# Attention and FFN on one core: side work dealt over the four head groups of a batch, units that cannot begin passed over, and norms moved to ScalarE

## The chip, the core and the metric

The kernel runs on one core of a Trainium2 chip. A core has TensorE (PE in the profile; PEld is its weight load), VectorE (DVE), ScalarE (ACT), GpSimd (POOL) and SyncE (SP, which here only issues transfers). Each engine runs its own instructions in the order in which they were issued, and waits on semaphores for the others. The metric is the device time of one execution in microseconds (us), as the median of several runs.

## What is computed

The reference works on four batches of 1024 rows with 256 columns, in float32, and on a context of 77 rows for each batch:

```python
x = x + xattn(_layernorm(x), ctx, Wq, Wkv, Wout, bout)   # 16 heads of 16, causal after the 77 context rows
x = x + ffn(_layernorm(x), w_fc, b_fc, w_proj, b_proj)

# xattn: q = x @ Wq; k, v = split(concat(ctx, x) @ Wkv)
#        softmax(q k^T / 4, keys j <= i + 77) @ v, then @ Wout + bout
# ffn:   every linear layer rounds its input and its weight to 3 mantissa bits with one
#        exponent per 32 columns; gelu between w_fc (1024 hidden) and w_proj
```

The keys are 77 + 1024 = 1101 for each batch.

## The kernel before, in words

**Head groups.** The sixteen heads of a batch are worked in four groups of four, so there are 16 groups, `kk` 0 to 15; batch `b` is groups 4b to 4b+3. A group is cut into 14 pieces of keys against queries: five for the first 512 queries (512, 461, 333, 205 and 77 columns wide) and nine for the second (512 five times, then 461, 333, 205, 77). Each piece is done in two half-steps of two heads each, so a group has 28 half-steps (`half_step`, L918). A half-step computes the raw scores of the *next* group for its row maxima (L490 on TensorE into `s_ps`, L514 or L516 on VectorE) and the transposed scores of *this* group (L554 into `st_ps`), whose exponential ScalarE takes (L565, `pt`); on the diagonal GpSimd zeroes the masked part (L570). The product with V (`times_v`, L591, `av_ps`) follows one to two half-steps behind. PSUM has two buffers of `st_ps` and three of `s_ps`.

**Side work.** All else is cut into units that are issued between half-steps. A unit is a list of stages; the first is issued at once, the others a given number of half-steps later (`begin` and `tick`, L891 and L901; `LATER` is 3). The units are:
- for the next batch: `load_unit`; `stats_unit` (L144, L145); `root1_unit` (Newton steps for 1/std, L160 to L163, on GpSimd); `norm_unit` (one tile: scale rows, L349, then turn on TensorE, L358, and copy into `xT`); `mem_unit` for the context; `qk_unit` and `v_unit` (projections, L420 and L393) and `move_unit` (transfers of a staged Q or K, L438, on SP's queue);
- for the batch before: `divide_unit` (softmax sums, transfers and L659); `wout_unit` (output projection L688, residual L696, statistics); `root_unit`; `in_unit` (norm L736, rounding with L178, L185, L189, L200, L201, turn L749); `hidden_unit` (four tiles of the first FFN layer, L768 to L779); `out_unit` (rounding, turn L820, projection L828, residual L835);
- in batch 0 sixteen `weight_unit` instead (rounding and turning the FFN weights, turn L858).

`helper[0]` is GpSimd from the first score step until the last group, and VectorE outside: it does the Newton steps, both norms, the residual additions, the scaling by the softmax sums and half of the rounding.

**Who decides the order.** `run` (L945) gets the group's list of units, written out by hand for each group of a batch (L999 to L1038). Each unit has a guessed cost; the list's total, spread over the half-steps by their width, gives a share for each, and the head of the list is issued while the share lasts and the unit's `ready()` holds:

```python
while todo and share > 0 and ready(todo[0]):
    u = todo.popleft()
    share -= price(u)
    begin(u)
```

What is left over is carried to the next group. In a batch that has both a batch before and one after it, group 0 got `wout` of the first half, Q and all norms of the next batch; group 1 the `in` units and the first `hidden`; group 2 five V units, four `out` units and Q, with K carried in from the group before; group 3 the rest.

Of the kernel before, what the change touches and what calls it, by code (L numbers as in the profile page):

```python
# [9 lines left out]
F32 = mybir.dt.float32  # L10
# [7 lines left out]
P = 128  # L18
# [7 lines left out]
ICW = 512  # L26
# [17 lines left out]
def kernel(  # L44
# [101 lines left out]

    def inv_std(mv, rstd, t0, t1, engine):


        n = t1 - t0  # L150
        v = small.tile([P, n], F32, name="v")
        nc.vector.tensor_scalar(v, mv[:, t0:t1, 1], EPS, None, ALU.add)
        y = small.tile([P, n], F32, name="y")
        nc.vector.tensor_scalar(
            y.bitcast(I32), v.bitcast(I32), -0.5, float(0x5F3759DF), ALU.mult, ALU.add
        )
        e = small.tile([P, n], F32, name="e")
        def newton(step):
            def emit():
                engine.tensor_tensor(e, y, y, ALU.mult)  # L160
                engine.tensor_tensor(e, e, v, ALU.mult)
                engine.tensor_scalar(e, e, -0.5, 1.5, ALU.mult, ALU.add)
                engine.tensor_tensor(y if step < 2 else rstd[:, t0:t1], y, e, ALU.mult)  # L163
            return emit

        return [newton(step) for step in range(3)]
# [38 lines left out]
    mv1 = const.tile([P, TT, 2], F32, name="mv1")  # L205
    rstd1 = const.tile([P, TT], F32, name="rstd1")
    mv2 = const.tile([P, TT, 2], F32, name="mv2")
    rstd2 = const.tile([P, TT], F32, name="rstd2")

    with ExitStack() as actx:
# [99 lines left out]
        def stats_unit(b, it):  # L312
            def emit():
                stats(xn[b, it // HN][:, it % HN, :], mv1, b * NT + it)
            return cost(0.7, emit)

        rooted1 = set()

        def root1_unit(b, half):
            got = {}  # L320

            def start():
                t0, n = (0, NT) if half is None else (half * HN, HN)
                got["steps"] = inv_std(mv1, rstd1, b * NT + t0, b * NT + t0 + n, helper[0])

# [16 lines left out]
        def norm_unit(b, it):  # L342
# [3 lines left out]
            def scale_rows():  # L346
                held["xh"] += 1
                xh = work.tile([P, D], F32, name="xh")
                helper[0].tensor_scalar(  # L349
                    xh, xn[b, it // HN][:, it % HN, :], mv1[:, t, 0:1], rstd1[:, t : t + 1],  # L350
                    ALU.subtract, ALU.mult,
                )
                got["xh"] = xh
# [8 lines left out]

            scale_rows.ready = lambda: (b, it // HN) in rooted1 and held["xh"] < XH
            return cost(0.8, [scale_rows, turn])

        def mem_unit(b):
# [16 lines left out]

            fetch.ready = room("xh", XH)
            return cost(0.5, [fetch, turn])

        def v_unit(b, jt):
            def emit():
# [15 lines left out]
                )  # L404
            return emit

        def qk_unit(hh, which, part):

            def emit():
# [18 lines left out]
                projected[b] += lo + n == total  # L428
            return cost(1.0, emit)

        def move_unit(hh, which):

            def emit():
                into, n = (qTs, N) if which == "q" else (kTs, KEYS)
                GR = HPG * HD
                for i in range(2):
                    t = into[(hh * 2 + i) % NQK]
                    nc.sync.dma_start(out=t[0:P:2, :], in_=qk_st[which][i * GR : (i + 1) * GR, :])  # L438
                    if which == "q" and hh * 2 + i >= NQK:
                        nc.sync.dma_start(out=t[MXR:P:PAD, :], in_=t[MXR + 2 : P : PAD, :])  # L440
            return emit

        def batch_units(b):
# [6 lines left out]
            for half in range(2):  # L450
                units += [stats_unit(b, half * HN + i) for i in range(HN)]
                units += [root1_unit(b, half)]
                units += [norm_unit(b, half * HN + i) for i in range(HN)]
            return first, units + [mem_unit(b)]

        def v_units(b):
            return [v_unit(b, jt) for jt in range(NJ)]

# [252 lines left out]
        def root_unit(b, half):  # L711
            got = {}

            def start():
                got["steps"] = inv_std(
                    mv2, rstd2, b * NT + half * HN, b * NT + (half + 1) * HN, helper[0]
                )
# [11 lines left out]
        def in_unit(t):  # L729
            got = {}  # L730

            def quantize():
                done["begun"] += 1
                held["xq"] += 1
                xh = work.tile([P, D], F32, name="xh")
                helper[0].tensor_scalar(  # L736
                    xh, x2[t], mv2[:, t, 0:1], rstd2[:, t : t + 1], ALU.subtract, ALU.mult
                )
                got["xh"] = xh
# [20 lines left out]
        def hidden_unit(tiles):  # L760
# [23 lines left out]
            )  # L784
            return cost(1.4 * len(tiles), emit)

# [97 lines left out]
        late = deque()  # L884
        LATER = 3
        clock = [0]
        pending = []
# [57 lines left out]
        def run(kk, extras):  # L945
# [10 lines left out]
            for n in range(STEPS):  # L956
                for pair in range(2):
# [16 lines left out]
                    tick()  # L974
                    share = min(share + rate * length[n], 2.5)
                    if urgent and ready(urgent[0]):
                        begin(urgent.pop(0))
                    while todo and share > 0 and ready(todo[0]):
                        u = todo.popleft()
                        share -= price(u)  # L980
                        begin(u)
                if kk >= 0:
# [16 lines left out]
        for kk in range(last + 1):  # L999
            b, g = divmod(kk, NG)  # L1000
            f = b - 1
            extras, qs, loads, norms = [], [], [], []
            if kk % 2 == 0:
                if kk // 2 + 1 < pairs:
                    extras.append(move_unit(kk // 2 + 1, "k"))
                    qs = q_units(kk // 2 + 1)
            if g == 0 and b + 1 < B:
                loads, norms = batch_units(b + 1)
            vs = v_units(b + 1) if b + 1 < B else []
            if g == NG - 1:  # L1010
                urgent += [divide_unit(b, 0), divide_unit(b, 1)]
            if f >= 0:
                T = range(f * NT, (f + 1) * NT)
                if g == 0:
                    extras += loads + wout_units(f, 0) + qs + [root_unit(f, 0)]
                    extras += norms + wout_units(f, 1) + [root_unit(f, 1)]
                elif g == 1:
                    extras += [in_unit(t) for t in T[:HN]] + [hidden_unit(T[:HN])]
                    extras += [out_unit(T[0])] + [in_unit(t) for t in T[HN:]]
                elif g == 2:  # L1020
                    extras += merge(vs[:5], [out_unit(t) for t in T[1:HN]]) + qs
                    extras += [hidden_unit(T[HN:])]
                else:
                    extras += merge(vs[5:], [out_unit(t) for t in T[HN:]])
            else:
                n = -(-len(w_units) // NG)
                side = w_units[g * n : (g + 1) * n]
                if g == 0:
                    extras += loads + side[:2] + qs + norms + side[2:]
                else:  # L1030
                    extras += side[:2] + qs + side[2:]
                    extras += vs[:5] if g == 2 else vs[5:] if g == 3 else []
            if kk % 2 == 1:
                if (kk + 3) // 2 < pairs:
                    extras += k_units((kk + 3) // 2)
            if kk == last:
# [52 lines left out]
```

## Time and profile before

| what | value |
|---|---|
| runs shown | 1061.28, 1061.05, 1059.31 us; median 1061.05 |
| profiled execution | 1055.06 us, span 1053.3 us |
| mean granted TensorE clock in it | 0.95 |
| before the first exponential | 66.7 us |
| groups 0 to 3 | 50.2, 52.8, 51.6, 51.8 us |
| groups 4 to 7 | 57.3, 61.5, 70.3, 57.4 us |
| groups 8 to 11 | 58.6, 59.2, 70.3, 57.0 us |
| groups 12 to 15 | 48.5, 61.8, 57.3, 40.2 us |
| after the last exponential | 80.8 us |

A group is measured from its first exponential (L565) to the next group's first. In the page's slices each digit is the busy share of one fortieth of the span in tenths; the row PEclk is the TensorE clock that was granted, in tenths of full speed. A row of a window shows start and end, length, then the busy time of each engine with its instruction count, the granted clock, the share of the DMA engines and GB/s. A line of a timeline has start, duration, engine, line, operation, output and inputs; the bracket at its end is the time the engine was idle before it and what released it. Group lines have the total busy time, the mean in nanoseconds, and the idle time ahead of them.

### The profile page before, as it was taken

What the parts mean: (1) busy time and instruction counts of PE and PEld (TensorE: products, weight loads), DVE (VectorE), ACT (ScalarE), POOL (GpSimd) and SP (SyncE); (2) the same over time, 40 slices, a digit from 0 to 9 for tenths busy, and PEclk for the clock granted to TensorE, in tenths of its full rate; (3) what the DMA queues carried; (4) which work ended last, traced back from release to release, by engine and by line L of the source; (5) the groups of instructions that cost most, each with busy time, mean ns of one, the idle gap of its engine ahead of it and who ended that gap; (6) DMA issues with size and microseconds to landing.
All of it is one profiled execution on the core that took longest, in us unless ns stands there. A gap on an engine that the chain in (4) does not pass through costs nothing.

```text
span 1053.3 us, 21100 instructions
## 1 busy us (share of the span) xinstructions
PE 974.8 (93%) x8024; PEld 408.7 (39%) x8024; DVE 653.0 (62%) x2121; ACT 544.3 (52%) x790; POOL 412.3 (39%) x775
## 2 busy tenths in 40 slices
PE   4899899999998999999998999999999898999577
PEld 2353334343433434344443434434443333344233
DVE  3678657655674756457566566646566756552695
ACT  5145445555554565655553564565554564756233
POOL 1014513131327446334326546515333627343233
PEclk9889989999997999999998999999999999989686
DMA  3030101101320001100320101010022000001200
GB/s 104 22 81 21 36 12 40 43 18 35 87 53 16 22 1 35 33 17 21 84 73 13 31 6 30 17 32 19 26 70 63 13 1 13 12 17 49 69 20 21
DMA packets 36172, 36.31 MB, mean 34 GB/s; under 512 B 14067, under 2 KB 29747, under 8 KB 36070
## 3 DMA queue, kind: packets, MB, share of 16 engines
q1 hardware_dynamic: 34958, 33.90, 11.8%
q8 instruction: 63, 1.03, 0.4%
q10 hardware_dynamic: 1112, 1.06, 0.3%
q14 instruction: 39, 0.32, 0.1%
HBM read 16.58 MB, written 5.25 MB: 21 GB/s over the span
## 4 chain that ended last, share of the span: by engine, by line
PE 75%; DVE 11%; POOL 5%; DMA 3%; ACT 2%; issue 2%; SPq 1%; POOLq 0%; DVEq 0%; ACTq 0%
PE s_ps L490 32%; PE av_ps L591 15%; PE s_ps L420 6%; PE st_ps L554 5%; PE s_ps L393 3%; PE st_ps L768 3%; DVE jk L516 3%; PE s_ps L688 3%; PE s_ps L828 2%; DVE mx L514 2%; PE st_ps L773 2%; ACT pt L565 2%; POOL xh L349 1%; DMA xn<-in_x_dram 1%; DVE amaxh L178 1%
## 5 line engine op out<-in xcount | busy, mean ns | idle before, releaser
L565 ACT ACTIVATE pt<-st_ps 128x1024 f32<-128x1024 f32 (+4 forms) x448 | 353.4, 793 | 303.8 <-PE st_ps L554 272.7
L490 PE MATMUL s_ps<-kT,qT 32*128 32x512 f32 (+2 forms) x1736 | 490.1, 543 | 21.5 <-DVE mxp L516 11.4
L554 PE MATMUL st_ps<-qT,kT 32*128 32x512 f32 (+5 forms) x1792 | 488.1, 540 | 2.5 <-ACT pt L565 2.4
L570 POOL TENSOR_SCALAR_AFFINE_SELECT pt<-pt 128x254 f32<-128x254 f32 (+3 forms) x320 | 118.1, 372 | 437.6 <-ACT pt L565 435.1
L516 DVE CUSTOM_DVE_ANT_0 jk<-s_ps,tri,mx 128x77 bf16<-128x77 f32 (+3 forms) x372 | 174.1, 505 | 154.3 <-PE st_ps L554 119.4
L490 PEld LDWEIGHTS s_ps<-kT,qT 32*128 32x128 f32 x1736 | 187.9, 189 | 208.3 <-issue 63.9
L591 PE MATMUL av_ps<-pt,vaug 128*32 128x256 f32 (+7 forms) x3072 | 226.1, 369 | 2.4 <-POOL hq L201 1.2
L514 DVE TENSOR_REDUCE mx<-s_ps 128x1 f32<-128x512 f32 x248 | 159.8, 685 | 78.3 <-PE st_ps L554 75.7
L554 PEld LDWEIGHTS st_ps<-qT,kT 32*128 32x128 f32 (+1 forms) x1792 | 182.5, 186 | 15.1 <-ACT pt L565 11.1
L516 DVE CUSTOM_DVE_ANT_0 jk<-s_ps,tri 128x512 bf16<-128x512 f32 (+3 forms) x248 | 126.6, 550 | 94.4 <-PE st_ps L554 74.4
L591 PEld LDWEIGHTS av_ps<-pt,vaug 128*32 128x32 f32 (+1 forms) x3072 | 62.6, 109 | 198.0 <-issue 137.2
L201 POOL TENSOR_TENSOR hq<-h,magh 128x512 bf16<-128x512 f32 x64 | 68.3, 1070 | 34.5 <-DVE h L200 28.9
L200 POOL TENSOR_TENSOR h<-h,magh 128x512 f32<-128x512 f32 x40 | 41.9, 1047 | 36.6 <-DVE magh L189 36.1
L673 ACT COPY y<-s_ps 128x256 f32<-128x256 f32 x64 | 23.9, 373 | 51.2 <-PE s_ps L692 26.2
L779 ACT ACTIVATE h<-st_ps 128x1024 f32<-128x1024 f32 x32 | 32.7, 1023 | 29.2 <-PE st_ps L773 29.1
L768 PE MATMUL st_ps<-wfcT,xqT 128*128 128x512 bf16 x128 | 44.7, 436 | 1.8 <-ACT xqT L752 1.8
L178 DVE TENSOR_REDUCE amaxh<-h 128x16 f32<-128x512 f32 x64 | 42.7, 675 | 5.4 <-ACT h L779 5.4
L420 PE MATMUL s_ps<-xT,wk_sb 128*128 128x512 f32 (+1 forms) x96 | 38.9, 533 | 5.2 <-DVE mxp L516 5.0
L516 DVE DVE_READ_ACCUMULATOR2_ANT mxp<- 128x1 f32 x512 | 42.2, 82 | 0.0
L688 PE MATMUL s_ps<-wo_sb,o_pk 128*128 128x256 f32 x128 | 38.2, 421 | 1.9 <-DVE o_pk L659 1.9
L393 PE MATMUL s_ps<-wv,xT 128*128 128x256 f32 (+1 forms) x144 | 38.0, 396 | 0.0
L828 PE MATMUL s_ps<-wprT,hT 128*128 128x256 bf16 x256 | 35.2, 283 | 2.7 <-ACT hT L823 2.6
(101 smaller groups left out, 817.6 us busy)
## 6 DMA issues: line engine op xcount, KB each, us to landing
kT<-k_st SPq DMA_DIRECT2D x16, 275.2 KB
xn<-in_x_dram SPq DMA_DIRECT2D x16, 256.0 KB
qT<-q_st SPq DMA_DIRECT2D x16, 256.0 KB
o_pk<-o_st SPq DMA_DIRECT2D x32, 128.0 KB
rb<-rd SPq DMA_DIRECT2D x128, 32.0 KB
x<-in_x_dram SPq DMA_DIRECT2D x32, 128.0 KB
out_dram<-x SPq DMA_DIRECT2D x32, 128.0 KB
x<-in_L_ffn_w_fc_dram SPq DMA_DIRECT2D x8, 128.0 KB
```

What stands on the lines that cost most here:

```text
L201: nc.gpsimd.tensor_tensor(dst.rearrange("p (n k) -> p n k", k=QBLK), src3, magb, ALU.subtract)
L393: nc.tensor.matmul(vp[:nj, :], xT[b][:, k, jt * P : jt * P + nj], wv[:, k, :], start=(k == 0), stop=(k == KC - 1),)
L420: nc.tensor.matmul(pp[:, :n], w[:, k, hi * P : (hi + 1) * P], xT[b][:, k, first + lo : first + lo + n], start=(k == 0), stop=(k == KC - 1),)
L490: nc.tensor.matmul(sp[:, 0 : hi - lo], qTs[kk % NQK][rows, it * P : (it + 1) * P], kTs[kk % NQK][rows, lo:hi], start=True, stop=True,)
L514: nc.vector.tensor_reduce(into, sp[:, 0:w], axis=AX.X, op=ALU.max)
L516: nc.vector.tensor_tensor_reduce(junk.tile([P, ICW], BF16, name="jk")[:, 0:w], sp[:, 0:w], mask, 1.0, before, ALU.add, ALU.max, into)
L554: nc.tensor.matmul(st[:nj, e, : i1 - i0], kTs[kk % NQK][rows, t * P : t * P + nj], qTs[kk % NQK][rows, i0:i1], start=True, stop=True,)
L565: nc.scalar.activation(pt[:nj, :, :w], st[:nj, :, :w], AF.Exp, scale=scale)
L570: nc.gpsimd.affine_select(out=pt[:nj, :, :behind], in_=pt[:nj, :, :behind], compare_op=ALU.is_ge, fill=0.0, base=base, pattern=[[0, 2], [1 ...
L591: nc.tensor.matmul(acc[c * PAD : (c + 1) * PAD, off + lo : off + hi], vaugs[b % 2][:nj, t, v0 : v0 + PAD], pts[kk, n, c // 2][:nj, c % 2, ...
L688: nc.tensor.matmul(yp, o_pk[b, ic][:, k, it * P % ICW : it * P % ICW + P], wo_sb[:, k, :], start=(k == 0), stop=False,)
L768: nc.tensor.matmul(hp[:, n, :], xqT[t][:, k, :], wfcT[:, k, n * ICW : (n + 1) * ICW], start=(k == 0), stop=False,)
```

## The change

It has three parts.

1. **Norms.** Where the helper is GpSimd, both norms become one ScalarE activation with a per-row scale (1/std) and a per-row shift (-mean/std). The root units compute the shift with two more small instructions in their last step. Where the helper is VectorE (ahead of the first score step and after the last group has begun), the norm stays as it was, and the two instructions are still issued.
2. **`run`.** Among the first four units of the list the first that is ready is issued, and at most 1.3 of guessed cost is issued in a half-step. The guessed costs change. Q and K units got a `ready()` of their own, over a staging state for each of Q and K, and the norms and the context of the next batch wait for the last Q or K projection of the batch before, since `xT` has one buffer.
3. **The lists.** Group 0 of a batch now has K and Q of its second half of the heads, `wout` of the first half, the norms of the first half of the next batch, the first root and the first four `in` units, and `wout` of the second half; group 1 has the first `hidden`, the norms of the second half, two `out` units and the second root; group 2 has K and Q of the next batch's first heads, two `out` units, four `in` units and the second `hidden`; group 3 has all nine V units and four `out` units.

The diff, cut:

```diff
             def emit():
                 engine.tensor_tensor(e, y, y, ALU.mult)
                 engine.tensor_tensor(e, e, v, ALU.mult)
                 engine.tensor_scalar(e, e, -0.5, 1.5, ALU.mult, ALU.add)
                 engine.tensor_tensor(y if step < 2 else rstd[:, t0:t1], y, e, ALU.mult)
+                if step == 2:
+                    engine.tensor_tensor(e, mv[:, t0:t1, 0], rstd[:, t0:t1], ALU.mult)
+                    engine.tensor_scalar(shift[:, t0:t1], e, -1.0, None, ALU.mult)
...
+    def norm(dst, src, mv, rstd, shift, t):
+        if helper[0] is nc.vector:
+            nc.vector.tensor_scalar(
+                dst, src, mv[:, t, 0:1], rstd[:, t : t + 1], ALU.subtract, ALU.mult
+            )
+        else:
+            nc.scalar.activation(
+                dst, src, AF.Identity, bias=shift[:, t : t + 1], scale=rstd[:, t : t + 1]
+            )
...
-                helper[0].tensor_scalar(
-                    xh, xn[b, it // HN][:, it % HN, :], mv1[:, t, 0:1], rstd1[:, t : t + 1],
-                    ALU.subtract, ALU.mult,
-                )
+                norm(xh, xn[b, it // HN][:, it % HN, :], mv1, rstd1, shift1, t)
...
-            scale_rows.ready = lambda: (b, it // HN) in rooted1 and held["xh"] < XH
+            scale_rows.ready = lambda: (
+                (b, it // HN) in rooted1 and held["xh"] < XH and (not b or projected[b - 1] == 2 * KC)
+            )
...
-            return cost(1.0, emit)
+                staged[which] = hh, part + 1
+            emit.ready = lambda: normed[hh // KC] == NT + 1 and (
+                staged[which] == (hh, part) if part else staged[which] is None
+            )
+            return cost(1.5, emit)
...
-                helper[0].tensor_scalar(
-                    xh, x2[t], mv2[:, t, 0:1], rstd2[:, t : t + 1], ALU.subtract, ALU.mult
-                )
+                norm(xh, x2[t], mv2, rstd2, shift2, t)
...
-            return cost(1.4 * len(tiles), emit)
+            return cost(0.8 * len(tiles), emit)
...
+        AHEAD = 4
...
                     share = min(share + rate * length[n], 2.5)
+                    left = 1.3
                     if urgent and ready(urgent[0]):
                         begin(urgent.pop(0))
-                    while todo and share > 0 and ready(todo[0]):
-                        u = todo.popleft()
+                    while share > 0 and left > 0:
+                        u = next((u for u in list(todo)[:AHEAD] if ready(u)), None)
+                        if u is None:
+                            break
+                        todo.remove(u)
                         share -= price(u)
+                        left -= price(u)
                         begin(u)
...
                 if g == 0:
-                    extras += loads + wout_units(f, 0) + qs + [root_unit(f, 0)]
-                    extras += norms + wout_units(f, 1) + [root_unit(f, 1)]
+                    extras += loads + merge(qs, wout_units(f, 0)) + norms[0][: HN + 1]
+                    extras += norms[0][HN + 1 :] + [root_unit(f, 0)] + ins[:HN]
+                    extras += wout_units(f, 1)
                 elif g == 1:
-                    extras += [in_unit(t) for t in T[:HN]] + [hidden_unit(T[:HN])]
-                    extras += [out_unit(T[0])] + [in_unit(t) for t in T[HN:]]
+                    extras += [hidden_unit(T[:HN])] + norms[1][: HN + 1]
+                    extras += merge(outs[:2], norms[1][HN + 1 :]) + [root_unit(f, 1)]
                 elif g == 2:
-                    extras += merge(vs[:5], [out_unit(t) for t in T[1:HN]]) + qs
-                    extras += [hidden_unit(T[HN:])]
+                    extras += merge(qs, outs[2:HN]) + ins[HN:] + [hidden_unit(T[HN:])]
                 else:
-                    extras += merge(vs[5:], [out_unit(t) for t in T[HN:]])
+                    extras += merge(vs, outs[HN:])
```

`qs` is now the K units, the K move, the Q units and the Q move of the same pair of heads; before, the K units of a pair stood at the end of the list of the group before.

## The prediction

> **What bounds the kernel now.** I read the page first (busy shares, slices, the chain that ended last), then busy time in windows cut at the first exponential (L565) of each of the sixteen head groups, then the timeline where a window showed TensorE idle. From the page:
>
> ```profile
> PE 974.8 (93%) x8024; PEld 408.7 (39%) x8024; DVE 653.0 (62%) x2121; ACT 544.3 (52%) x790; POOL 412.3 (39%) x775
> PE   4899899999998999999998999999999898999577
> PEclk9889989999997999999998999999999999989686
> PE 75%; DVE 11%; POOL 5%; DMA 3%; ACT 2%; issue 2%; SPq 1%; POOLq 0%; DVEq 0%; ACTq 0%
> ```
>
> TensorE carries three quarters of the chain and its work is the same before and after, so only its stalls can be won: the idle slots, and the slices where the granted clock (PEclk) drops. Windows of head groups 4, 5, 6, 7, 8, 12 and 13 (start:end, length, busy us of PE, PEld, DVE, ACT, POOL, then granted clock):
>
> ```profile
> 273.10:330.40 57.30, 53.76 (x456) 21.53 (x452) 37.14 (x130) 27.11 (x41) 25.56 (x64) 0.93 0.22 58
> 330.40:391.90 61.50, 59.72 (x483) 23.08 (x478) 37.23 (x127) 33.77 (x50) 28.80 (x58) 0.95 0.06 17
> 391.90:462.20 70.30, 67.49 (x564) 28.80 (x556) 38.11 (x121) 40.68 (x58) 34.65 (x51) 1.00 0.11 28
> 462.20:519.60 57.40, 55.72 (x520) 24.51 (x512) 36.04 (x116) 31.34 (x46) 26.39 (x40) 1.00 0.09 25
> 519.60:578.20 58.60, 55.03 (x456) 21.66 (x452) 38.91 (x130) 27.09 (x41) 25.64 (x64) 0.92 0.25 67
> 764.70:813.20 48.50, 48.36 (x452) 19.78 (x444) 32.51 (x110) 25.73 (x36) 17.14 (x40) 1.00 0.27 70
> 813.20:875.00 61.80, 57.43 (x480) 22.09 (x476) 37.43 (x128) 33.19 (x45) 29.40 (x56) 0.92 0.02 7
> ```
>
> Group 12 is nearly stall-free (0.14 us idle, full clock). Its side work is two Q units at 1.93 us (the chain has 1.91 to 1.98) and four output projections at 1.2 (38.2 us / 32): 8.7. So a bare group is 48.5 - 8.7 = 39.8 us. Other TensorE prices: V unit 1.06 (38.0 / 36), hidden unit of four tiles 6.5 (its half-step lasts 8.1 instead of 1.6), out unit 1.75 (turn 0.7, project 1.05), norm turn 0.4, quantised turn 0.29, 77-column K part 0.4. Bare group plus its units, against its length, gives each group's stall: groups 0 to 3: 2.4, 7.0, 1.4, 2.3; 4 to 7: 7.2, 7.3, 2.4, 2.1; 8 to 11: 8.5, 5.0, 2.4, 1.7; 12 to 14: 0, 8.8, 3.5. Together 62 us: some 31 idle, some 21 lost to the clock ((1 - granted) x length), the rest half-steps stretched by VectorE. This is all the change can reach; the first 66.7 us and all after group 14 change little.
>
> Two places show how stalls arise (start, duration, engine, line, what; in brackets idle before and releaser):
>
> ```profile
> 317.95 4.83 POOL L349 TENSOR_SCALAR xh<-xn,mv,rstd 128x256 f32<-128x256 f32 x4
> 320.43 0.44 PE L358 MATMUL s_ps<-ident,xh 128*128 128x128 f32 x2 [0.78 <-POOL xh L349]
> 321.63 0.44 PE L358 MATMUL s_ps<-ident,xh 128*128 128x128 f32 x2 [0.76 <-POOL xh L349]
> 322.84 0.69 PE L358 MATMUL s_ps<-ident,xh 128*128 128x128 f32 x2 [0.76 <-POOL xh L349]
> ...
> 395.40 2.42 POOL L736 TENSOR_SCALAR xh<-x,mv,rstd 128x256 f32<-128x256 f32 x2
> 396.65 0.42 DVE L178 TENSOR_REDUCE amaxx<-xh 128x8 f32<-128x256 f32 x1 [0.71 <-POOL xh L736]
> 399.43 1.98 PE L420 MATMUL s_ps<-xT,wk_sb 128*128 128x512 f32 x4 [2.48 <-DVE mxp L516]
> ```
>
> First TensorE itself waits for GpSimd's norms, 1.2 us apiece. Then VectorE, in order, waits for a norm with maxima queued behind it; score buffers stay full and TensorE loses 2.48 us.
>
> **Part 1: the norms.** 48 norms (24 L349, 24 L736) leave GpSimd for ScalarE:
>
> ```profile
> L736 POOL TENSOR_SCALAR xh<-x,mv,rstd 128x256 f32<-128x256 f32 x24 | 29.2, 1219 | 0.0
> L565 ACT ACTIVATE pt<-st_ps 128x410 f32<-128x410 f32 x64 | 32.7, 515 | 28.8 <-PE st_ps L554 20.8 <-POOL pt L570 6.2 <-POOL hq L201 1.5
> L673 ACT COPY y<-s_ps 128x256 f32<-128x256 f32 x64 | 23.9, 373 | 51.2 <-PE s_ps L692 26.2 <-PE s_ps L831 24.7
> ```
>
> GpSimd loses 58 us and gains two small instructions in each of 12 roots: 24 at 0.28 us spacing, 7. ScalarE gains 48 activations. The near row, a 256-column copy, says 0.37 us each, 18 in all. [...] ScalarE then works some 55% of the time, so the amount is hidden behind TensorE. The built program has 14 table loads in both versions: none added.
>
> The price is the new wait. A norm needs the root's last step on GpSimd, now six instructions, 1.7 us, and is often issued in the same half-step. Behind it in ScalarE's queue stand the next exponential, and behind that TensorE, which has two score tiles. Group 4 has two such places. In its wide half-step 8 the root started one and a half half-steps earlier and two residual additions (0.72 each) share GpSimd: ScalarE waits 0 to 1.9 us, then runs three norms (1.7); the slack is about 1.2, so TensorE loses 0 to 2.4; I take 1.2. In half-step 10 the mask select L570 (0.42) stands ahead of the root step and itself waits for the exponential: wait 2.2, norms 1.1 to 2.2, cost 1 to 3, I take 2. Group 8 repeats this; group 12 has one place with a 1.27 us scaling ahead as well (2.5); groups 0 and 1 one each (1).
>
> **Part 2: a unit that cannot begin is passed over; even dealing.** The second half's norms, wout and `in` units move from groups 5 and 6 forward to 4 or are spread out; K, Q and V projections gather in groups 0, 2 and 3 of each batch. Their DMAs move with them: a K or Q move on SP is now issued after its staging is complete, twenty or more us ahead of its first reader, so SP's maxima transfers queued behind wait no longer than now. Costed at nothing; if that cover went, a late mask row would stop the scores.
>
> TensorE's sum is unchanged, but where it stands matters. Without side work the first half-steps (from one L554 start to the next) last 1.56, 0.96, 2.2, 0.92, 2.37, 1.34: the long ones wait for VectorE (two 512-column maxima, 1.5 us). A projection issued ahead of a long one hides in that wait: in group 12, half-steps 5 to 7 cost 15.2 us where bare (10.0) plus units (6.2) make 16.2. The change puts projections at 0 and 1 in groups 4, 5, 6, 8, 9, 10, 12: 0.9 to 1.8 us each, some 9 in all.
>
> Against it: group 4 quantises four tiles in its narrow last half-steps. GpSimd has two 1.27 us scalings and four roundings at 1.23 there, about 8 us with selects, where TensorE needs 5: by itself 3.3 us; the same sum for group 4 as it is gives 3.2 where 2.35 of idle is seen, so I take 2.0. Group 5's four statistics (0.6 each) and a quantise stand at 5 to 7 without TensorE work: 2.5.
>
> **The clock.** Group 8 around the burst of statistics (same columns):
>
> ```profile
> 553.80:557.60 3.80, 2.75 (x20) 0.76 (x16) 3.60 (x15) 1.08 (x2) 1.04 (x5) 1.00 0.26 52
> 557.60:564.40 6.80, 6.80 (x40) 2.11 (x40) 4.04 (x12) 2.51 (x3) 3.86 (x19) 0.53 0.06 10
> ```
>
> 1.05 us of idle is followed by 6.8 us at half clock, 3.4 lost. [...] The row decides; about half the stalls above 1 us here drew such a window, so I add 1.5 us each.
>
> **The sum**, new stalls. Group 4: 1.0 (statistics) + 1.2 + 2.0 + 2.0 + clock 3.0 - 1.8 = 7.4, no better than 7.2. Group 5: 2.0 (2.5, clock and remnants, less 1.8), was 7.3. Group 6: 0.5, was 2.4: the rounding that VectorE waited for is gone. Group 7: 2. Groups 4 to 7 make 12, were 19.0: 7 won; 8 to 11 win 5.6; 12 to 14 make 1.8 + 4.2 + 2.5 = 8.5, were 12.3: 3.8. Groups 0 to 3 make 9, were 13.1: 4. Ahead of group 0 the V units spread out between maxima: 1.3. The two shift instructions on VectorE at the start and in the tail cost 0.4. Net 21 us. The profiled execution took 1055.06 (span 1053.3); 1034 there. The shown runs' median is 6 higher, 1061.05: 1040.
>
> **Rivals.** *The new ScalarE waits win (slower).* Ten places hang on GpSimd's queue (three each in groups 4 and 8, two in 12, one each in 0 and 1). I charge 26 us for them with their clock windows. At full price, 2.2 wait + 1.7 norms - 1.2 slack + 3.4 clock = 6.1 each, they take 61: 14 us slower, 1075. It decides from 4.7 us a place; just beyond is 1066. For: GpSimd's select waits for ScalarE, and ScalarE then for GpSimd. Against: GpSimd is 58 us lighter. Chance 0.20.
> *Stalls only change places.* TensorE's work is conserved, VectorE is close behind it in wide half-steps, and dealing work to another group moves idle time: 1050 to 1062, centre 1057. Chance 0.15.
> *Clean.* No place costs over 1 us and the clock holds in groups 0 to 14: 62 less 15 left, 47 won: 1014. Chance 0.13.
> Likeliest, 0.52: 1040, own range 1028 to 1050.
>
> **Numbers.** Range 1020 to 1068: it leaves out most of the clean case and the dear half of the slow one. 0.2% (2 us) is about what a measurement can tell from no change. Faster 0.73 (likeliest, clean, half the third), same 0.06, slower 0.21.
>
> **What would show it.** Right: no waits of PE or DVE on xh; group 5 near 57 us, 13 near 57; GpSimd near 360 us busy, ScalarE near 570. Wrong: ACT rows waiting for POOL shift over 2 us in groups 4, 8, 12, followed by PEclk near 0.5; group 4 above 65 us; or an unchanged total clock loss of 21 us in groups 0 to 14.

## The result and the profile after

The changed kernel takes 1049.33 us (median of 4 runs, 1048.25 to 1050.89) where the kernel before took 1060.59 beside it: ratio 0.9896, 95% interval 0.9879 to 0.9913, 11.3 us faster. Run again later beside other kernels it had 0.9907 (0.9874 to 0.9940). The forecast was 1040: the direction was right, the gain about half of what was forecast. The profiled execution took 1048.25 us (span 1046.5). Its counterpart of before was 6 us under its own median, so the two spans differ by only 6.8 us. The rows below explain those 6.8, not the 11.3; ratios are always of timed runs of one set, because the kernel before itself had medians of 1055 to 1061 us from set to set.

The same four rows of the page as in the prediction: busy shares, TensorE's busy tenths, its granted clock, the chain that ended last.

```profile
PE 981.6 (94%) x8024; PEld 416.2 (40%) x8024; DVE 652.6 (62%) x2127; ACT 564.9 (54%) x838; POOL 360.0 (34%) x751
PE   4899999999999999999998999999998999999677
PEclk9899999999998999999998999999997899989576
PE 79%; DVE 9%; ACT 3%; DMA 2%; POOL 2%; issue 2%; SPq 1%; POOLq 0%; ACTq 0%; DVEq 0%
```

GpSimd lost 52 us, as forecast (360), and ScalarE gained 21, a little less than forecast (565 instead of 570). GpSimd's part of the chain fell from 5% to 2%. TensorE's busy row has fewer dips, but its clock row still has them. "Half clock" below is time in which the granted clock was 0.5 of full speed. TensorE's own busy time even rose by 6.8 us, with the same instructions. Over the whole span the time at half clock rose from 106 to 113 us; a matmul at half clock counts as busy for longer (one of 32x512 on L518 for 1.12 us in the half clock from 319.4 to 329.5, for 0.66 from 329.6 to 380, means), which by the 7 us more of half clock makes an estimated 3 of the 6.8. The rest is not explained. The windows of groups 4, 5, 8, 9, 12 and 13, columns as before:

```profile
264.40:326.00 61.60, 58.70 (x476) 24.77 (x472) 39.46 (x132) 32.82 (x55) 25.12 (x64) 0.95 0.20 52
326.00:385.90 59.90, 57.65 (x503) 23.62 (x498) 37.05 (x127) 36.45 (x53) 23.21 (x55) 0.97 0.04 10
506.20:569.20 63.00, 60.09 (x485) 25.58 (x481) 39.46 (x132) 33.27 (x57) 25.84 (x65) 0.94 0.26 70
569.20:628.00 58.80, 57.23 (x503) 23.41 (x495) 37.02 (x127) 36.44 (x53) 23.13 (x55) 0.98 0.03 10
748.30:806.60 58.30, 55.77 (x469) 23.07 (x465) 37.30 (x124) 29.06 (x45) 20.76 (x47) 0.95 0.20 50
806.60:867.80 61.20, 60.62 (x502) 24.30 (x495) 35.26 (x115) 34.68 (x48) 22.63 (x46) 0.91 0.05 14
```

With the prediction's accounting (length less the bare group, less its units at their prices), the stalls became, in us (the last column adds up to 6.2; the other 0.6 is in rounding and unit prices):

| stage | before | forecast | after | gain forecast | gain measured |
|---|---|---|---|---|---|
| ahead of group 0 | | | | 1.3 | -1.7 |
| groups 0 to 3 | 13.1 | 9 | 7.2 | 4 | 5.9 |
| groups 4 to 7 | 19.0 | 12 | 15.4 | 7 | 3.6 |
| groups 8 to 11 | 17.6 | 12 | 14.6 | 5.6 | 3.0 |
| groups 12 to 14 | 12.3 | 8.5 | 14.5 | 3.8 | -2.2 |
| tail | | | | -0.4 | -2.4 |

The three longest gaps that are left stand at the ends of groups 4, 8 and 12; the half clock behind them reaches into groups 5, 9 and 13. From the first exponential of group 0 to that of group 15 TensorE's idle fell from 31.5 to 19.2 us, but its time at half clock only from 44.4 to 39.1. The end of group 12 in the timeline (start, duration, engine, line, what; in brackets idle before and releaser):

```profile
796.53 1.28 POOL L687 TENSOR_TENSOR o_pk<-o_pk,rb 128x512 f32<-128x512 f32 x1
...
799.18 0.22 POOL L168 TENSOR_SCALAR shift<-e 128x4 f32<-128x4 f32 x1
799.44 1.09 ACT L224 ACTIVATE xh<-x,shift,rstd 128x256 f32<-128x256 f32 x2 [3.37 <-POOL shift L168]
800.07 0.42 DVE L183 TENSOR_REDUCE amaxx<-xh 128x8 f32<-128x256 f32 x1 [1.72 <-ACT xh L224]
...
800.98 0.41 PE L582 MATMUL st_ps<-qT,kT 32*77 32x77 f32 x1 [2.54 <-ACT pt L593]
```

GpSimd has a 1.28 us scaling ahead of the root's last step. ScalarE waits 3.37 us for the shift, the next exponential stands behind its two norms, and TensorE waits 2.54 us for that exponential. Then the clock falls. The next two windows are this gap and what follows it; the granted clock is the third figure from the end:

```profile
798.40:800.90 2.50, 0.04 (x1) 0.00 (x0) 0.76 (x4) 1.46 (x4) 0.75 (x4) 0.93 0.00 0
800.90:818.00 17.10, 16.88 (x95) 7.29 (x99) 9.78 (x34) 7.46 (x15) 8.74 (x17) 0.51 0.04 11
```

A gap of 2.5 us is followed by 17.1 us at half clock, some 8.5 us of lost TensorE time. Groups 4 and 8 end alike, by another cause. The lines are group 4's; the last one of VectorE is the first of the score maxima that TensorE waits for:

```profile
315.87 1.27 POOL L687 TENSOR_TENSOR o_pk<-o_pk,rb 128x512 f32<-128x512 f32 x1
...
316.12 1.04 DVE L190 TENSOR_SCALAR magx<-amaxx 128x8 int32<-128x8 int32 x1
317.20 0.54 DVE L194 TENSOR_SCALAR magx<-magx 128x8 f32<-128x8 f32 x1
317.65 0.41 DVE L183 TENSOR_REDUCE amaxx<-xh 128x8 f32<-128x256 f32 x1
318.09 0.34 DVE L190 TENSOR_SCALAR magx<-amaxx 128x8 int32<-128x8 int32 x1
318.46 0.54 DVE L194 TENSOR_SCALAR magx<-magx 128x8 f32<-128x8 f32 x1
318.91 0.42 DVE L544 CUSTOM_DVE_ANT_0 jk<-s_ps,tri,mx 128x205 bf16<-128x205 f32 x1
...
319.39 0.49 PE L518 MATMUL s_ps<-kT,qT 32*128 32x77 f32 x1 [2.40 <-DVE mxp L544]
```

In VectorE's lines quantise steps, from 316.12 on, stand ahead of the maxima (318.91) that free TensorE's score tiles, and L190, 0.17 us in the median, takes 1.04 while GpSimd scales. TensorE idles 2.40 us (2.41 in group 8), and 10.2 us at half clock begin at the end of each gap or, in group 8, 0.9 us before it:

```profile
316.90:319.40 2.50, 0.10 (x3) 0.01 (x2) 2.40 (x8) 0.00 (x0) 2.34 (x5) 0.98 0.00 0
319.40:329.50 10.10, 10.10 (x61) 5.13 (x65) 2.73 (x14) 3.29 (x8) 5.44 (x11) 0.50 0.00 0
```

How long the half clock lasts is not fixed by the gap. In the profiled execution of the repeat the same three gaps (2.40, 2.40 and 2.51 us) had 6.8, 10.2 and 10.2 us of it; here is the one of group 12:

```profile
798.30:800.80 2.50, 0.01 (x1) 0.00 (x0) 0.82 (x4) 1.52 (x4) 0.69 (x4) 0.84 0.00 0
800.80:810.20 9.40, 9.38 (x60) 3.92 (x60) 6.29 (x22) 3.61 (x9) 7.61 (x14) 0.50 0.00 1
```

### The profile page after: what moved, and what is told of

Same layout as the page of the kernel before. It is cut to its first block, busy times and chain, and to the rows that moved or that the text cites. A ratio compares the mean times of both kernels' runs of the same rounds, so it can differ in the third digit from the quotient of the medians.

```text
span 1046.5 us, 21087 instructions
## 1 busy us (share of the span) xinstructions
PE 981.6 (94%) x8024; PEld 416.2 (40%) x8024; DVE 652.6 (62%) x2127; ACT 564.9 (54%) x838; POOL 360.0 (34%) x751
## 4 chain that ended last, share of the span: by engine, by line
PE 79%; DVE 9%; ACT 3%; DMA 2%; POOL 2%; issue 2%; SPq 1%; POOLq 0%; ACTq 0%; DVEq 0%
PE s_ps L518 35%; PE av_ps L619 16%; PE s_ps L441 6%; PE st_ps L582 5%; PE s_ps L412 3%; PE st_ps L794 3%; PE s_ps L716 3%; DVE jk L544 3%; PE s_ps L854 2%; PE st_ps L799 2%; ACT pt L593 2%; DVE mx L542 1%; PE s_ps L846 1%; DVE amaxh L183 1%; PE s_ps L373 1%
## 5 line engine op out<-in xcount | busy, mean ns | idle before, releaser
L518 PE MATMUL s_ps<-kT,qT 32*128 32x512 f32 (+2 forms) x1736 | 491.8, 537 | 15.0 <-DVE mxp L544 8.2
L582 PE MATMUL st_ps<-qT,kT 32*128 32x512 f32 (+5 forms) x1792 | 482.4, 534 | 7.4 <-ACT pt L593 6.9
L518 PEld LDWEIGHTS s_ps<-kT,qT 32*128 32x128 f32 x1736 | 194.5, 187 | 189.8 <-issue 70.5
L619 PE MATMUL av_ps<-pt,vaug 128*32 128x256 f32 (+7 forms) x3072 | 223.8, 365 | 2.4 <-POOL hq L206 1.2
L542 DVE TENSOR_REDUCE mx<-s_ps 128x1 f32<-128x512 f32 x248 | 159.4, 683 | 85.6 <-PE st_ps L582 70.3
L582 PEld LDWEIGHTS st_ps<-qT,kT 32*128 32x128 f32 (+1 forms) x1792 | 186.5, 184 | 21.2 <-ACT pt L593 17.8
L701 ACT COPY y<-s_ps 128x256 f32<-128x256 f32 x64 | 23.9, 374 | 49.7 <-PE s_ps L720 24.4
L183 DVE TENSOR_REDUCE amaxh<-h 128x16 f32<-128x512 f32 x64 | 42.7, 675 | 5.4 <-ACT h L805 5.4
L716 PE MATMUL s_ps<-wo_sb,o_pk 128*128 128x256 f32 x128 | 42.5, 459 | 1.6 <-DVE o_pk L687 1.6
L412 PE MATMUL s_ps<-wv,xT 128*128 128x256 f32 (+1 forms) x144 | 40.9, 410 | 1.0 <-DVE mx L542 1.0
```

The source lines that it names most:

```text
L412: nc.tensor.matmul(vp[:nj, :], xT[b][:, k, jt * P : jt * P + nj], wv[:, k, :], start=(k == 0), stop=(k == KC - 1),)
L518: nc.tensor.matmul(sp[:, 0 : hi - lo], qTs[kk % NQK][rows, it * P : (it + 1) * P], kTs[kk % NQK][rows, lo:hi], start=True, stop=True,)
L542: nc.vector.tensor_reduce(into, sp[:, 0:w], axis=AX.X, op=ALU.max)
L582: nc.tensor.matmul(st[:nj, e, : i1 - i0], kTs[kk % NQK][rows, t * P : t * P + nj], qTs[kk % NQK][rows, i0:i1], start=True, stop=True,)
L619: nc.tensor.matmul(acc[c * PAD : (c + 1) * PAD, off + lo : off + hi], vaugs[b % 2][:nj, t, v0 : v0 + PAD], pts[kk, n, c // 2][:nj, c % 2, ...
L716: nc.tensor.matmul(yp, o_pk[b, ic][:, k, it * P % ICW : it * P % ICW + P], wo_sb[:, k, :], start=(k == 0), stop=False,)
```

## Experiments

All ratios are to the kernel before in the same set. Idle and half clock are TensorE's in groups 0 to 14 of the profiled execution; the last column is the time that ScalarE's norms waited for GpSimd's shift, and how many waited.

| kernel | ratio, 95% interval | median us | idle | half clock | wait for shift |
|---|---|---|---|---|---|
| before | 1 | 1060.59 | 31.5 | 44.4 | |
| changed | 0.9896, 0.9879 to 0.9913 | 1049.33 | 19.2 | 39.1 | 8.9, 4 |
| changed, again | 0.9907, 0.9874 to 0.9940 | 1045.24 | 20.1 | 32.3 | 8.9, 4 |
| dealing alone | 0.9960, 0.9939 to 0.9980 | 1054.29 | 24.5 | 49.6 | |
| norms alone | 0.9984, 0.9963 to 1.0004 | 1054.60 | 26.3 | 50.7 | 11.9, 5 |
| no passing over | 1.0068, 1.0049 to 1.0088 | 1064.35 | 25.6 | 59.8 | 18.2, 6 |
| late turns | 0.9859, 0.9816 to 0.9902 | 1042.98 | 22.5 | 23.8 | 8.9, 4 |
| late marks | 0.9714, 0.9688 to 0.9740 | 1025.57 | 10.0 | 4.8 | 3.0, 3 |
| norms twice | 1.0107, 1.0069 to 1.0145 | 1067.20 | 33.7 | 54.4 | 8.9, 4 |
| tiles dealt to the next group | 0.9880, 0.9850 to 0.9909 | 1042.27 | 19.8 | 32.3 | 6.1, 3 |
| first roots' marks late | 0.9909, 0.9877 to 0.9941 | 1049.49 | 17.2 | 51.2 | 9.0, 3 |
| late marks, norms twice | 0.9896, 0.9864 to 0.9929 | 1046.66 | 19.7 | 15.4 | 3.1, 3 |
| late marks, GpSimd norms | 0.9917, 0.9885 to 0.9949 | 1051.70 | 20.1 | 49.6 | |
| late marks, VectorE norms | 0.9818, 0.9780 to 0.9855 | 1039.70 | 13.1 | 12.1 | |

### The parts by themselves

The dealing and the passing over, without the norms' move (the shift instructions leave the root too):

```diff
-        if helper[0] is nc.vector:
-            nc.vector.tensor_scalar(
...
+        helper[0].tensor_scalar(
+            dst, src, mv[:, t, 0:1], rstd[:, t : t + 1], ALU.subtract, ALU.mult
+        )
```

> The changed kernel with its lists and its passing over, but every norm back on GpSimd (one fused subtract and multiply, no shift instructions): the second and third part of the change alone. Theory A (my prediction: the norms' move and the dealing each win several us): GpSimd goes back to about 415 us busy, TensorE and VectorE wait for GpSimd's xh again, ScalarE's 8.9 us of waits for shift go; 1054 to 1060 us. Rival B (the dealing alone makes the gain, the norms' move is worth nothing or less): 1045 to 1050 us, no slower than the changed kernel's 1049. Rival C (stalls only change places, and what was won is won in the granted clock): anything from 1045 to 1060, with the sum of half-clock time in groups 0 to 14 carrying the difference.

The kernel before with the norms on ScalarE (the `norm` function and the shift instructions of the change, nothing else of it):

> The kernel before, with its own lists, costs and order of issue, and only the norms on ScalarE with scale and shift: the first part of the change alone. Theory A: the waits of TensorE on GpSimd's xh in groups 4 and 8 and of VectorE's amax on it in group 6 and 10 go (some 5 to 8 us of idle), ScalarE's waits for shift give a part back; 1052 to 1057 us. Rival B: 1059 to 1062 us, the same as before. Rival C: the total moves less than 3 us, with idle down and half-clock time up.

Measured 0.9960 and 0.9984, against 0.9896 and 0.9907 for the whole. Theory A holds for the dealing alone (1054.29, just inside its 1054 to 1060) and B falls for it. For the norms alone A's 1052 to 1057 us holds in absolute time, but the kernel before ran 1057.85 in that set: the ratio cannot be told from no change, as B said, and idle falls by 5 us while half clock rises by 6, as C said. So no gain can be told for the norms moved to ScalarE by themselves: TensorE's idle falls, ScalarE waits 11.9 us for the shift, and about 3 us more are lost at half clock.

### Without the passing over

```diff
-        AHEAD = 4
+        AHEAD = 1
```

> The changed kernel, but only the first unit of the list may begin (AHEAD is 1): a unit that cannot begin holds up all behind it, as before. Theory A (projections issued ahead of VectorE's long half-steps hide there, which needs the passing over where a unit waits for a root or a buffer): 1052 to 1058 us, with work bunched at the ends of groups 4, 8 and 12. Rival B2 (the even lists alone do it; the passing over is hardly used): 1048 to 1051 us.

Measured 1.0068: dearer than A thought, and slower than the kernel before. The even lists need the passing over; with them it is worth 1.6 to 1.7%. The wait for the shift doubles (the row is engine, line, what it waits for, then total us, times, longest):

```profile
ACT xh L224 <- POOL shift L168: 18.2, 6, 4.8
```

### Turns later

```diff
-            return cost(1.2, [quantize, (2, rounding), turn])
+            return cost(1.2, [quantize, (2, rounding), (6, turn)])
```

> The changed kernel with the turn of each quantised tile issued six half-steps after its rounding's mark instead of the usual three. It takes away TensorE's wait for GpSimd's roundings at the ends of groups 4 and 8 (13.1 us of waits on xq in the changed kernel, the longest 7.8). Theory A (these waits and the half clock behind them are what the prediction missed in groups 4, 5, 8 and 9): those waits fall under 3 us, groups 4 and 8 shorten by 3 to 5 us each, 1038 to 1044 us. Rival C (the work the turn holds up, the hidden units, only moves to a later place and waits there): groups 7 and 11 grow by what 4 and 8 lose, 1047 to 1051 us.

Measured 0.9859, some 0.4% below the changed kernel's two ratios, with intervals that overlap. Its 1042.98 us lies in A's band, but A's reason fails: 12.2 of the 13.1 us of waits on xq remain (they are two waits, the longest 7.8 us), and TensorE's 2.40 us of idle in groups 4 and 8 stays, since VectorE makes it. Groups 4 and 5 together are only 0.9 us shorter. The turn waiting for GpSimd was not what the narrow ends cost. In this profiled execution the gaps of 2.40, 2.40 and 2.51 us had 6.8 us at half clock each, less than in either execution of the changed kernel; whether the later turns or chance made them shorter is not shown.

### Norms later

A root now counts as ready two half-steps after its last step was issued, so ScalarE is given a norm when the shift is there:

```diff
-                    if n == 2:
-                        rooted.add(b * NT // HN + half)
...
+            def mark():
+                rooted.add(b * NT // HN + half)
...
-            return cost(0.5, [start, (1, step(0)), (1, step(1)), (1, step(2))])
+            return cost(0.5, [start, (1, step(0)), (1, step(1)), (1, step(2)), (2, mark)])
```

and the same for the first norm's roots. Beside it ran the changed kernel again:

> The changed kernel once more, beside the others of this set, since the kernel before ran some 3 us shorter in the first set of experiments than beside the changed kernel. Theory A: its ratio to the kernel before stays near 0.990 (0.987 to 0.993), and the places of its stalls in the trace are the same (groups 4, 8 and 12), so these belong to the program. Rival C (the gain is luck in the granted clock of that execution): a ratio of 0.994 or more, with the stalls elsewhere.

> The changed kernel, with each root counted as ready only two half-steps after its last step on GpSimd was issued, so that ScalarE's norms are issued when the shift is there. Theory A (ScalarE's waits for GpSimd and the half clock behind them cost about what the prediction charged, 1 to 2.5 us a place and the clock on top): the 8.9 us of waits for shift go to under 1, the 2.54 us of TensorE idle at the end of group 12 goes; ratio to the changed kernel 0.992 to 0.997, 3 to 8 us. Rival B3 (those waits are hidden but for group 12): 0.997 to 1.000. Rival C (the norms' turns and the quantised tiles, now later, stall the narrow half-steps instead): 1.000 or more.

The changed kernel's ratio was 0.9907 with the gaps in the same places (2.40, 2.40 and 2.51 us at the ends of groups 4, 8 and 12): they belong to the program. The late marks gave 0.9714, 1.9% below the changed kernel in the same set, 20 us where A expected 3 to 8, though the waits for the shift fell to 3.0 us and not under 1. The clock row of its page, and windows of groups 4, 5 and 12:

```profile
PEclk9899999999999999999999999999999999989576
```

```profile
268.00:321.90 53.90, 53.64 (x467) 22.06 (x464) 38.30 (x131) 31.90 (x51) 23.05 (x61) 1.00 0.20 52
321.90:381.80 59.90, 59.39 (x502) 24.52 (x503) 37.18 (x129) 37.66 (x57) 26.34 (x65) 1.00 0.06 17
731.90:785.60 53.70, 53.70 (x486) 22.45 (x481) 32.85 (x113) 28.10 (x41) 16.83 (x40) 1.00 0.23 58
```

Groups 4, 8 and 12 have hardly any idle left (0.26 us in group 4's window, none in group 12's), and beyond the first 80 us there is no gap over 0.7 us until group 15, and no half clock. Against the repeated changed kernel, idle in groups 0 to 14 falls by 10.1 us and half clock by 27.5 (13.7 of lost time); the groups are 18.0 us shorter, so not all of the two shows in the time. The delay does two things: ScalarE waits 3.0 us instead of 8.9, and the quantise steps that depend on the second root's norms slide later, two of the four tiles of groups 4, 8 and 12 into the first half-steps of the next group. The next two experiments try to take these apart.

### The quantised tiles moved, or half of the marks

The first moves the first four quantised tiles to the head of the next group's list. The second delays only the first norm's roots.

```diff
-                    extras += norms[0][HN + 1 :] + [root_unit(f, 0)] + ins[:HN]
+                    extras += norms[0][HN + 1 :] + [root_unit(f, 0)]
...
-                    extras += [hidden_unit(T[:HN])] + norms[1][: HN + 1]
+                    extras += ins[:HN] + [hidden_unit(T[:HN])] + norms[1][: HN + 1]
```

> The changed kernel with the first four quantised tiles of a batch dealt to the head of the next group's list (groups 5, 9, 13) in place of the last of groups 4, 8, 12. It takes four quantise steps, their roundings and turns out of the narrow half-steps at the ends of these groups. Theory A (the narrow ends are where the prediction's gain was lost: 2.4 us of idle on VectorE's maxima behind the quantise steps in groups 4 and 8, 2.5 on ScalarE behind the shift in 12, and 31 us at half clock after them): idle and half clock in groups 4, 5, 8, 9, 12 and 13 fall by more than half, ratio to the changed kernel 0.984 to 0.992, near 1037 us where that takes 1049. Rival C (stalls only change places): groups 5, 9 and 13 grow by what 4, 8 and 12 lose, ratio 0.996 to 1.004.

> The changed kernel with only the roots of the first norm (six of twelve) counted as ready two half-steps after their last step; the second norm's roots mark at once as in the changed kernel. With both late the ratio to the changed kernel was 0.981. Theory A2 (every place where ScalarE waits for the shift costs alike, by the idle and by the half clock it sets off): groups 4 and 8, which have one place of each kind, keep half of their loss, group 12 keeps all of it: ratio to the changed kernel 0.988 to 0.994. Rival E (only the second root's places count, since they push the quantise steps into the narrow half-steps): 0.997 to 1.002. Rival F (only the first root's count): 0.981 to 0.986 but for group 12's 5 us.

Tiles moved: 0.9880, 0.997 of the changed kernel; rival C. The 2.4 us gaps go, but gaps of 1.16 and 1.17 us on VectorE's maxima (between statistics and quantise steps) come in groups 5 and 9, with half clock after them:

```profile
335.84 0.33 PE L518 MATMUL s_ps<-kT,qT 32*128 32x77 f32 x1 [1.16 <-DVE mxp L544]
```

First roots late: 0.9909, no different from the changed kernel, as rival E said. But this kernel waits for the shift as long as the changed kernel does (9.0 us): the wait only moved to the second roots, so it does not show that the first roots' places are free. Neither part alone brings the 20 us; a kernel with only the second roots late was not run, so whether it alone would is open.

### Amount or wait

Each of ScalarE's norms issued twice, in the changed kernel and in that with late marks:

```diff
-            nc.scalar.activation(
-                dst, src, AF.Identity, bias=shift[:, t : t + 1], scale=rstd[:, t : t + 1]
-            )
+            for _ in range(2):
+                nc.scalar.activation(
+                    dst, src, AF.Identity, bias=shift[:, t : t + 1], scale=rstd[:, t : t + 1]
+                )
```

> The changed kernel with each of ScalarE's 48 norms issued twice (same result, 48 more activations of 0.59 us, 28 us). Theory A (the amount of ScalarE's work is hidden, only its waits count): ScalarE busy near 593 us, the time 0 to 4 us longer. Rival D (ScalarE's queue itself sets the time in the half-steps where the norms stand, since the next exponential waits behind them): 10 to 20 us longer, with TensorE's scores waiting on pt in groups 4, 5, 8, 9, 12.

> The changed kernel with both roots' marks two half-steps later, and each of ScalarE's norms issued twice, 28 us of ScalarE more. It tells the amount from the wait. Theory A2 (ScalarE's waits for the shift were the loss, and the amount is hidden where it does not wait): 0 to 5 us over the same kernel with single norms (ratio 0.971 to 0.976 to the kernel before). Rival D (the norms themselves, ahead of the next exponential in ScalarE's queue, are the loss; twice as many cost some 20 us as they did in the changed kernel): ratio to the kernel before 0.985 to 0.995.

Rival D both times, in the first a little past its 10 to 20 us: 1.0107 against 0.9907, 22 us (2.0%) longer, and 0.9896 against 0.9714 (of another set), 19 us (1.9%) longer, for 26 to 27 us more of ScalarE (busy 591.7 and 591.3). The waits of TensorE's transposed scores on the exponential, first of the changed kernel:

```profile
PE st_ps L582 <- ACT pt L593: 6.9, 9, 2.5
```

then with norms twice:

```profile
PE st_ps L583 <- ACT pt L594: 15.8, 14, 3.8
```

Up to three norms stand in a row ahead of the next exponential, and six where each is issued twice. ScalarE is busy 55 to 57% of the time, yet some three quarters of what is added in those places shows in the end.

### The norms' engine, once nobody waits for the shift

Late marks, with the norms on GpSimd or on VectorE (no shift instructions in either):

> The changed kernel with both roots' marks two half-steps later, and the norms on GpSimd as in the kernel before (no shift instructions). Theory A2 (the norms' move off GpSimd wins by itself once ScalarE does not wait): 6 to 14 us slower than the same kernel with the norms on ScalarE, ratio to the kernel before 0.977 to 0.985. Rival B (the late marks and the dealing make the gain, on whichever engine the norms are): within 3 us of it, 0.969 to 0.975.

> The changed kernel with both roots' marks two half-steps later, and the norms on VectorE (no shift instructions), where one should take 0.25 to 0.45 us. Theory A2 (VectorE is the engine that TensorE waits for in the wide half-steps, so 12 to 20 us more there shows in part): 3 to 10 us slower than with the norms on ScalarE, ratio to the kernel before 0.974 to 0.981. Rival G (a norm on VectorE is shorter and nothing queues ahead of the exponentials): the same or up to 5 us faster, 0.967 to 0.972.

GpSimd 0.9917, 2.1% above the late marks on ScalarE (whose 0.9714 is of another set); VectorE 0.9818, 1.1% above. A norm took 1.22 us on GpSimd and 0.44 to 0.47 (means) on VectorE. Both are slower than A2's bands (0.977 to 0.985, 0.974 to 0.981), the second barely; B and G fall. With GpSimd a chain as in the kernel before returns at the start of groups 5, 9 and 13:

```profile
318.93 2.44 POOL L216 TENSOR_SCALAR xh<-x,mv,rstd 128x256 f32<-128x256 f32 x2
320.19 0.42 DVE L180 TENSOR_REDUCE amaxx<-xh 128x8 f32<-128x256 f32 x1 [2.82 <-POOL xh L216]
...
323.83 1.22 PE L511 MATMUL s_ps<-kT,qT 32*128 32x512 f32 x1 [3.95 <-DVE mx L537]
```

So the move to ScalarE is worth 2% with the new lists and late marks, some 0.5 to 0.6% with the new lists alone (0.9896 and 0.9907 against 0.9960), and nothing that can be told in the lists of before.

## Why the prediction was right in its sign and half wrong in its size

- **Part 1, what leaves GpSimd.** Right. No wait of TensorE on GpSimd's xh is left, VectorE's is 1.7 us once, on ScalarE. A norm on ScalarE took 0.59 us, not the copy row's 0.37. The 1.7 us that the forecast has for three norms, its 1.1 to 2.2 and its 570 us of ScalarE rest on an estimate of mine that no run shows; in its place the runs showed 1.57 us for three in a row (the changed kernel, from 301.45 us) and 565 us in all:

```profile
L224 ACT ACTIVATE xh<-x,shift,rstd 128x256 f32<-128x256 f32 x24 | 13.8, 593 | 6.9 <-POOL shift L168 6.9
```

- **"the amount is hidden behind TensorE".** Wrong as a reason. Doubling it cost 19 to 22 us. I read ScalarE's share of the whole span, and the norms come up to three at a time ahead of one exponential. What the single norms cost is not shown, but they are not free.
- **The new waits.** Four waits of 8.9 us in all (groups 0, 4, 8 and 12), not ten places. My own counts disagree: the working prices seven places, the rival charges ten. Group 12's 2.5 us was measured as 2.54. What I called half-step 10 of group 4 (the eleventh piece, half-steps 20 and 21 of 28) was costed at 2: ScalarE waited 1.78 us, and TensorE lost 0.47.
- **"so I add 1.5 us each", for the clock.** This is the step that was mis-sized most. The gaps of 2.40, 2.41 and 2.54 us had 10.2, 10.2 and 17.1 us at half clock, up to 5.1 + 5.1 + 8.5 = 18.7 us lost, where I had 3.0 in group 4, 3.0 in group 8 and, at 1.5 a place, 1.5 in group 12: 11 us more, or 6 with the half clock of the repeated execution. 15 us are missing between 21 and 6, but the terms do not simply add up to that: groups 6 and 10 (5 us) and start and tail (5 us) were short too, and cheaper waits and groups 0 to 3 gave some back. The 1.5 was a fair mean of the kernel before: its nine gaps over 1 us had 27 us at half clock, 1.5 us lost for each. It hid the spread. Of its three gaps over 2.1 us the two of 2.48 in groups 6 and 10 had no half clock and the one of 2.36 in group 13 had 6.8 us; over all 14 executions 27 of 29 such gaps had some. That the trace of before holds the only two without was bad luck for this step.
- **Group 4's narrow end.** 2.0 forecast, 2.40 measured, by another mechanism: VectorE's maxima behind quantise steps, not TensorE's turn behind GpSimd. Making the turns later left the gap.
- **Groups 5, 6 and 10.** Groups 6 and 10 fell from 70.3 to 63.2 us. By the accounting all of that is unit work moved to other groups, and the stall was 3.0 us each, not 0.5; but TensorE was idle for only 0.6 us there and had full clock, so the unit prices or stretched half-steps are off. Group 5 had 4.4 instead of 2.0: 2.2 of idle and 3.5 us at half clock, which belong to the 10.2 above.
- **Start and tail.** Forecast +1.3 and -0.4, measured -1.7 and -2.4. The tail has the same order of instructions in both but for the four of the shift on VectorE, and 54.8 instead of 44.7 us at half clock. Over all other kernels it had 49.7 to 62.2, so the 44.7 is the odd one: the profiled execution of before was a quick one, 6 us under its median.
- **The signs named in advance.** Of those for right, the waits on xh went, GpSimd came to 360 us and ScalarE to 565; groups 5 and 13 had 59.9 and 61.2 us instead of 57. Of those for wrong, ScalarE waited over 2 us in group 12 (3.37) with half clock behind it, but 1.78 in groups 4 and 8; group 4 stayed under 65 us; and the loss to the clock in groups 0 to 14 was nearly unchanged, some 22 us before and 20 after.
- **Rivals.** "ScalarE waits win" fell: only group 12, with its clock, reached the price of 4.7 us. The 26 us that I charged to its places are still of the size of what the late marks give back (18 to 20), though part of that is the quantise steps' gap. "Stalls only change places" explains groups 12 and 13, and the measured 1049.33 is 0.7 us under its range, at the dear end of the likeliest's 1028 to 1050. That it lies in the latter is in part luck, since dearer clock and cheaper waits cancelled in part. The late marks, at 0.9714 of the 1061 us from which the 1014 us of the clean case was reckoned, stand at 1031, 17 us above it, so most of that gain was there to be won.

## What to carry to other kernels

Do not ask whether an engine has time over the whole span, but what stands behind a moved instruction in its queue and whether its inputs are there when it is issued: holding the norms back by two half-steps was worth more than the whole change, though the runs do not part the shorter wait from the quantise steps that moved with it. A gap in TensorE's work is to be priced with the half clock after it, and with its spread: gaps of 2.4 to 2.5 us lost from nothing (twice in the kernel before) to 8.5 us more. The stalls to remove first were those over 1 us here: 54 of 67 had half clock with them or close behind, of those of 0.7 to 1 us 11 of 27. Test a move with its engine's amount doubled: it tells hidden work from an engine that only looks idle (here 26 to 27 us more of ScalarE took 19 to 22 us).

## What the runs showed of the hardware

In groups 0 to 14 of the 14 profiled executions there were 65 periods at half clock, from 3.4 to 20.5 us long; the eight of the kernel before lasted 3.4, 6.8 or 10.2 us, the four of the changed kernel 3.4, 10.2, 10.2 and 17.1. Of TensorE's gaps there, 27 of 29 over 2.1 us had half clock within them or beginning up to 5 us behind them, 27 of 38 of 1 to 2.1 us, and 11 of 27 of 0.7 to 1 us, some of these close to a longer one; of moments taken at even steps over the same groups, 7% had it or were in it. The two long gaps without are those of 2.48 us in the kernel before. Six of the 65 periods had no gap over 0.15 us in the 7 us before them; what set them off the traces do not show.

VectorE's L190 (128x8 and 128x32) took 0.17 to 0.18 us in the 21 cases of groups 4 to 14 of the changed kernel in which GpSimd ran nothing beside it, and 1.04 to 1.12 in the three that met the scaling L687. In the lines shown it ends at 317.16, the scaling at 317.14. Where it met a shorter instruction of GpSimd that had begun before it (0.61 us), it took 0.34 to 0.48 us and again ended 0.03 us after it; the reduction L183 kept its 0.41 us beside them. What holds L190 the runs do not show.
